# Layer 0 of a two-layer attention network: scores and values in groups of two steps, and the embedding's terms in one matmul

## The chip, the cores and the metric

The kernel runs on one core of one Trainium2 chip. The metric is the device time of one execution in microseconds (us); the time of a kernel is the median of its runs, and less is better. A core has a matmul engine (TensorE, "PE" in the profile, its weight loads listed apart as "PEld"), a vector engine (VectorE, "DVE"), an activation engine (ScalarE, "ACT"), a general engine (GpSimd, "POOL") and a queue that issues transfers (SyncE, "SP"). They run side by side and wait for one another through semaphores. SBUF is the working memory of 128 partitions; PSUM holds the results of matmuls, here in 8 banks of 128 x 512 float32.

## The reference

Two layers work on an input of 2 x 512 channels x 64 x 32 positions, that is 2048 positions per batch. Layer 0, the only one that the change touches, is softmax attention with 8 heads of 64 channels. Queries and keys get 64 extra input channels (32 that depend on the row alone, 32 that depend on the column alone):

```python
def _L0_conv_ref(hidden_states, Wq, Wk, Wv, Wout, bout):
    emb = get_embeddings(B, H, W, FREQ_DIM, TIME_DIM, ...)   # 32 rows of freq (by h), 32 of time (by w)
    qk_hs = jnp.concatenate([hidden_states, emb], axis=1)
    ...
    q = qk_hs @ Wq ; k = qk_hs @ Wk ; v = v_hs @ Wv          # 8 heads of 64
    scores = jnp.einsum('bhqd,bhkd->bhqk', q, k) * scale
    attn = jax.nn.softmax(scores, axis=-1)
    o = jnp.einsum('bhqk,bhkd->bhqd', attn, v)
    o = o @ Wout + bout
    return o + hidden_states
```

Layer 1 (a landmark attention with a pseudo-inverse, a convolution of 33 taps and a dequantised linear layer) follows, and takes more than half of the time. Its instructions are the same before and after the change. All arithmetic is float32.

## The kernel before

Layer 0 walks over 8 pairs of heads (2 batches x 4 pairs). For one pair, `q` and `k` lie in SBUF as 128 rows (64 per head) x 2048 positions, `v` as 16 tiles of 128 positions x 128. One step is a pair (t, c): t is one of 4 blocks of 512 queries, c one of 16 tiles of 128 keys, so there are 64 steps per pair and 512 in the layer. A step makes the scores of both heads, 64 rows of TensorE each, into one PSUM tile of two banks (two such tiles), and ScalarE's exponential into an SBUF tile `p` (4 buffers). The values part of the step multiplies `p` by `v`, 64 columns of TensorE for each head, into `av`, and VectorE adds `p` to `acc`, from which the sums of the softmax come at the end of a block of queries. The values of a step are issued after the scores of the next:

```python
ps      = tile_pool(bufs=2, space=PSUM)     # sc: 2 x 2 banks, av: 2 x 1, pp: 2 x 1
ppool   = tile_pool(name="pf0", bufs=4)     # p, and the squares of the layer norm
...
def scores(t, c):
    sc = ps.tile([P, 2, TB], F32, tag="sc")
    for h in range(2):
        rows = slice(h * D, (h + 1) * D)                       # D = 64
        nc.tensor.matmul(sc[:, h, :], lhsT=hd.k[rows, c * P : (c + 1) * P],
                         rhs=hd.q[rows, t * TB : (t + 1) * TB], start=True, stop=True)   # L881
    p = ppool.tile([P, 2, TB], F32, tag="p")
    nc.scalar.activation(p, sc, AF.Exp, scale=D**-0.5)                                   # L889
    return p

for i in range(len(steps) + 1):
    p = scores(*steps[i]) if i < len(steps) else None
    if pending is not None:
        (t, c), pp = pending
        if c == 0:
            av = ps.tile([P, TB], F32, tag="av"); acc = apool.tile([P, 2, TB], F32, tag="acc")
        for h in range(2):
            half = slice(h * D, (h + 1) * D)
            nc.tensor.matmul(av[half, :], lhsT=hd.v[:, c, half], rhs=pp[:, h, :],
                             start=c == 0, stop=c == NST - 1)                            # L903
        if c == 0: first = pp
        else:      nc.vector.tensor_tensor(acc, first if c == 1 else acc, pp, ALU.add)   # L909
        if c == NST - 1:
            rs = bank(...)                                                 # two matmuls, L913
            nc.vector.reciprocal(rinv, rs)                                               # L917
            nc.vector.tensor_tensor(hd.q[:, t * TB : (t + 1) * TB], av, rinv, ALU.mult)  # L918
    pending = (steps[i], p) if p is not None else None
    while done * len(steps) < n_filler * (i + 1) and next(filler, filler) is not filler:
        done += 1
```

The fillers are pieces of other work, so that they lie between steps: 15 units that make `q`, `k` and `v` of the next pair of heads, and, while the first pair of batch 1 runs, 24 units that finish batch 0 (output projection `yp` and layer norm). The projections use the whole 128 x 128 array:

```python
fp = bank(...)                                      # the embedding's terms
nc.tensor.matmul(fp[:, :H], lhsT=we[kind][:, 0, cols], rhs=femb, ...)           # 32 rows, L756
nc.tensor.matmul(fp[:, H:H + W], lhsT=we[kind][:, 1, cols], rhs=temb, ...)      # 32 rows, L757
...                                                 # DVE copy, POOL spreads the sum over 64 x 32
for k in range(KC):                                 # 4 matmuls per 512 positions, L773
    nc.tensor.matmul(pp, lhsT=w_sb[kind][:, k, cols], rhs=xbs[t][:, k, :], ...)
nc.vector.tensor_tensor(dst[:, toks], pp, e[:, toks], ALU.add)                  # L776
...
mean  = matmul(mean_w, total)                       # finish: L841, after POOL's sums (L814)
xn    = xb - mean                                   # DVE, L843
sq    = POOL: squares and their sum                 # L849 to L851, two buffers of ppool
var   = matmul(mean_w, sq)                          # L854
rstd  = apool.tile([P, TB], F32, tag="rstd", bufs=1)   # ACT Sqrt, DVE reciprocal, POOL product
```

The scheduler of the language may move an instruction ahead of its neighbours on the same engine; it did so for some scores, whose two heads then stand apart.

Of the kernel before, what the change touches and what calls it, by code (L numbers as in the profile page):

```python
# [10 lines left out]
F32 = mybir.dt.float32  # L11
I32 = mybir.dt.int32
AF = mybir.ActivationFunctionType
ALU = mybir.AluOpType
AX = mybir.AxisListType

P = 128
B, C, H, W = 2, 512, 64, 32
S = H * W
KC = C // P  # L20
HEADS, D = 8, 64
NPAIR = HEADS // 2
TB = 512
NTB = S // TB
NST = S // P
# [628 lines left out]

SAFE = 60.0


@with_exitstack
def layer0(
# [20 lines left out]
    nc = tc.nc  # L680
    const = ctx.enter_context(tc.tile_pool(name="const0", bufs=1))
    small = ctx.enter_context(tc.tile_pool(name="small0", bufs=2))
    ps = ctx.enter_context(tc.tile_pool(name="ps0", bufs=2, space=bass.MemoryType.PSUM))
    wpool = ctx.enter_context(tc.tile_pool(name="wf0", bufs=1))
# [1 line left out]
    epool = ctx.enter_context(tc.tile_pool(name="ef0", bufs=1))  # L686
    qopool = ctx.enter_context(tc.tile_pool(name="qof0", bufs=NPAIR + 1))
    kvpool = ctx.enter_context(tc.tile_pool(name="kvf0", bufs=2))
    ppool = ctx.enter_context(tc.tile_pool(name="pf0", bufs=4))
    apool = ctx.enter_context(tc.tile_pool(name="af0", bufs=2))  # L690
    lpool = ctx.enter_context(tc.tile_pool(name="lf0", bufs=1))

# [3 lines left out]
    def bank(name):  # L696
        return ps.tile([P, 512], F32, tag="pp", name=name)
# [3 lines left out]
    ones = const.tile([P, D], F32, name="ones_f")  # L701
# [9 lines left out]
    nc.sync.dma_start(b0_sb, b0)  # L711
    bound = const.tile([P, B * NPAIR], F32, name="bound0")

    femb = const.tile([32, H], F32, name="femb")
    nc.sync.dma_start(femb, freq)
    temb = const.tile([32, W], F32, name="temb")
    nc.sync.dma_start(temb, time)
    w_sb, we = {}, {}
    for kind, w in (("q", wq0), ("k", wk0)):
        w_sb[kind] = wpool.tile([P, KC, C], F32, name=f"w{kind}_f")  # L720
        nc.sync.dma_start(w_sb[kind], chunked(w[:C, :]))
        we[kind] = wpool.tile([32, 2, C], F32, name=f"we{kind}_f")
        nc.sync.dma_start(we[kind], w[C:, :].rearrange("(s p) n -> p s n", p=32))

    def load_x(b):
        tiles = []
# [12 lines left out]
    class Heads:  # L739
# [6 lines left out]
        def units(self):  # L746
            cols = slice(self.hp * P, (self.hp + 1) * P)
            xbs = self.xbs
            self.q = qopool.tile([P, S], F32, tag="qo", name=f"q_{self.name}")
            self.k = kvpool.tile([P, S], F32, tag="k", name=f"k_{self.name}")  # L750
            self.v = kvpool.tile([P, NST, P], F32, tag="v", name=f"v_{self.name}")

            def embedded(kind):

                fp = bank(f"fp_{kind}_{self.name}")
                nc.tensor.matmul(fp[:, :H], lhsT=we[kind][:, 0, cols], rhs=femb, start=True, stop=True)  # L756
                nc.tensor.matmul(fp[:, H : H + W], lhsT=we[kind][:, 1, cols], rhs=temb, start=True, stop=True)  # L757
                ft = small.tile([P, H + W], F32, tag="ft", name=f"ft_{kind}_{self.name}")
                nc.vector.tensor_copy(ft, fp[:, : H + W])
                e = epool.tile([P, H, W], F32, tag="e", name=f"e_{kind}_{self.name}")  # L760
                nc.gpsimd.tensor_tensor(
                    e,
                    ft[:, :H].unsqueeze(2).to_broadcast([P, H, W]),
                    ft[:, H:].unsqueeze(1).to_broadcast([P, H, W]),
                    ALU.add,
                )
                return e.rearrange("p h w -> p (h w)")

            def project(kind, dst, e, t):
                toks = slice(t * TB, (t + 1) * TB)  # L770
                pp = bank(f"pp_{kind}_{self.name}_{t}")
                for k in range(KC):
                    nc.tensor.matmul(  # L773
                        pp, lhsT=w_sb[kind][:, k, cols], rhs=xbs[t][:, k, :], start=k == 0, stop=k == KC - 1
                    )
                nc.vector.tensor_tensor(dst[:, toks], pp, e[:, toks], ALU.add)  # L776

            def values(t):
                vp = bank(f"vp_{self.name}_{t}")
                for j in range(4):  # L780
                    for k in range(KC):
                        nc.tensor.matmul(
                            vp[:, j * P : (j + 1) * P],
                            lhsT=xbs[t][:, k, j * P : (j + 1) * P],
                            rhs=wv_sb[:, k, cols],
                            start=k == 0,
                            stop=k == KC - 1,
                        )
                nc.scalar.copy(self.v[:, 4 * t : 4 * t + 4, :], vp.rearrange("p (j d) -> p j d", d=P))

            for kind, dst in (("q", self.q), ("k", self.k)):
                e = embedded(kind)
                yield
                for t in range(NTB):
                    project(kind, dst, e, t)
                    yield
            for t in range(NTB):
                values(t)
                yield

            big = small.tile([P, 2], F32, tag="big", name=f"big_{self.name}")
            for i, m in enumerate((self.q, self.k)):
                nc.vector.tensor_reduce(big[:, i : i + 1], m, AX.X, ALU.max, apply_absolute_value=True)
            i = self.b * NPAIR + self.hp
            nc.vector.tensor_tensor(bound[:, i : i + 1], big[:, :1], big[:, 1:], ALU.mult)
            yield
# [10 lines left out]
    def finish_units(b, oTs):  # L817

        for t in range(NTB):
            toks = slice(t * TB, (t + 1) * TB)  # L820
            name = f"f0_{b}_{t}"
            xb = lpool.tile([P, KC, TB], F32, tag="xr", name=f"xr_{name}")
            nc.sync.dma_start(xb, chunked(x[b])[:, :, toks])
            for m in range(KC):
                yp = bank(f"yp_{name}_{m}")
                for k in range(NPAIR):
                    nc.tensor.matmul(
                        yp,
                        lhsT=wo_sb[:, k, m * P : (m + 1) * P],
                        rhs=oTs[k][:, toks],  # L830
                        start=k == 0,
                        stop=k == NPAIR - 1,
# [19 lines left out]
            var = bank(f"var_{name}")  # L852
            for j in range(2):
                nc.tensor.matmul(var, lhsT=mean_w, rhs=sq[:, j, :], start=j == 0, stop=j == 1)  # L854
            rstd = apool.tile([P, TB], F32, tag="rstd", name=f"rstd_{name}", bufs=1)
            nc.scalar.activation(rstd, var, AF.Sqrt, bias=eps, scale=1.0)
            nc.vector.reciprocal(rstd, rstd)
            nc.gpsimd.tensor_tensor(
# [13 lines left out]
    def attention(hd, filler, n_filler):  # L872

        steps = [(t, c) for t in range(NTB) for c in range(NST)]
        av, acc, done = None, None, 0

        def scores(t, c):
            sc = ps.tile([P, 2, TB], F32, tag="sc", name=f"sc_{hd.name}_{t}_{c}")
            for h in range(2):
                rows = slice(h * D, (h + 1) * D)  # L880
                nc.tensor.matmul(  # L881
                    sc[:, h, :],
                    lhsT=hd.k[rows, c * P : (c + 1) * P],
                    rhs=hd.q[rows, t * TB : (t + 1) * TB],
                    start=True,
                    stop=True,
                )
            p = ppool.tile([P, 2, TB], F32, tag="p", name=f"p_{hd.name}_{t}_{c}")
            nc.scalar.activation(p, sc, AF.Exp, scale=D**-0.5)  # L889
            return p  # L890

        pending = None
        first = None
        for i in range(len(steps) + 1):
            p = scores(*steps[i]) if i < len(steps) else None
            if pending is not None:
                (t, c), pp = pending
                if c == 0:
                    av = ps.tile([P, TB], F32, tag="av", name=f"av_{hd.name}_{t}")
                    acc = apool.tile([P, 2, TB], F32, tag="acc", name=f"acc_{hd.name}_{t}")  # L900
                for h in range(2):
                    half = slice(h * D, (h + 1) * D)
                    nc.tensor.matmul(  # L903
                        av[half, :], lhsT=hd.v[:, c, half], rhs=pp[:, h, :], start=c == 0, stop=c == NST - 1
                    )
                if c == 0:
                    first = pp
                else:
                    nc.vector.tensor_tensor(acc, first if c == 1 else acc, pp, ALU.add)  # L909
                if c == NST - 1:  # L910
                    rs = bank(f"rs_{hd.name}_{t}")
                    for h in range(2):
                        nc.tensor.matmul(  # L913
                            rs[h * D : (h + 1) * D, :], lhsT=ones, rhs=acc[:, h, :], start=True, stop=True
                        )
                    rinv = apool.tile([P, TB], F32, tag="rinv", name=f"rinv_{hd.name}_{t}", bufs=1)
                    nc.vector.reciprocal(rinv, rs)  # L917
                    nc.vector.tensor_tensor(hd.q[:, t * TB : (t + 1) * TB], av, rinv, ALU.mult)  # L918
            pending = (steps[i], p) if p is not None else None
            while done * len(steps) < n_filler * (i + 1) and next(filler, filler) is not filler:  # L920
                done += 1
        for _ in filler:
            pass
# [137 lines left out]
```

## Time and profile before

| | |
|---|---|
| time, median of 3 runs | 4262.48 us (4260.63 to 4263.36) |
| span of the profiled execution | 4266.9 us |
| TensorE matmuls, busy | 3966.1 us, 93% |
| VectorE, ScalarE, GpSimd, busy | 42%, 26%, 8% |
| scores (L881), values (L903), records | 2048 each |
| exponentials (L889) | 512, 1024 ns each |
| additions to `acc` (L909) | 448 of 1320 ns mean |

The page gives the busy time of each engine, the chain of work that ended last, and groups of instructions by line. A float32 matmul shows as two records of TensorE, each about half of its work, so a pair of heads has four records per step. Two matmuls on different rows or columns of the array may have records that start together. The end of a record is modelled, so the time that TensorE spends on something is read from the start of one record to the start of the next. In the timeline the columns are the start, the length, engine, line, operation, output and inputs, the part of the array (rows*columns) and the shape, the number of records merged, and in brackets the idle time ahead and who ended it.

### The profile page before, as it was taken

How to read it: one execution, taken by the hardware profiler on the slowest of the kernel's cores; microseconds unless marked ns; L12 is line 12 of the kernel's file. 1: busy time of each engine (PE TensorE's matmuls, PEld its weight loads, DVE VectorE, ACT ScalarE, POOL GpSimd, SP SyncE). 2: the span in 40 equal slices, each digit the busy share in tenths (PEclk: the TensorE clock that was granted, in tenths of full speed). 3: DMA queues.
4: the chain of work that ended last, by engine and by line, in shares of the span. 5: the costliest groups of instructions: out<-in, count | busy, mean ns of one | idle time of the engine just before them, and what ended most of it. 6: DMA issues, size and time to landing. Idle time of an engine off the chain costs nothing.

```text
span 4266.9 us, 42948 instructions
## 1 busy us (share of the span) xinstructions
PE 3966.1 (93%) x18002; PEld 2285.3 (54%) x18002; DVE 1808.6 (42%) x2393; ACT 1113.8 (26%) x1760; POOL 326.8 (8%) x200
## 2 busy tenths in 40 slices
PE   8999999989999995379999999899999789999987
PEld 3333233323332322258888888577677347677743
DVE  3565655565555562463333333224323214323322
ACT  1333333322333440012212211123223103223210
POOL 1000000132000004530000000000000100000001
PEclk9999999999999997679999999899999999999999
DMA  2000010010000002300000000100010010000010
GB/s 92 1 1 1 1 40 1 30 59 30 1 1 1 1 1 89 90 0 1 1 1 1 1 1 1 62 1 8 1 50 30 30 35 8 8 1 1 11 50 31
DMA packets 48970, 81.92 MB, mean 19 GB/s; under 512 B 3584, under 2 KB 22016, under 8 KB 48768
## 3 DMA queue, kind: packets, MB, share of 16 engines
q1 hardware_dynamic: 42240, 53.92, 3.9%
q0 software_dynamic: 6528, 25.17, 1.6%
q8 instruction: 144, 2.36, 0.2%
q14 instruction: 58, 0.48, 0.0%
HBM read 52.34 MB, written 26.74 MB: 19 GB/s over the span
## 4 chain that ended last, share of the span: by engine, by line
PE 80%; issue 9%; POOL 4%; DVE 3%; DMA 1%; ACT 1%; SPq 0%; POOLq 0%; ACTq 0%; DVEq 0%
PE sc_f L881 10%; PE av_f L903 9%; PE pr_a L437 4%; PE pr_b L437 4%; PE pr_c L437 4%; PE pr_z L437 4%; PE acc L599 4%; PE sc L113 3%; PE sc L568 3%; PE pp_q_f L773 3%; PE acc L607 3%; PE av L134 3%; PE pp_q L169 3%; PE vp L183 3%; PE pp_k L169 3%
## 5 line engine op out<-in xcount | busy, mean ns | idle before, releaser
L909 DVE TENSOR_TENSOR acc_f<-acc_f,p_f 128x1024 f32<-128x1024 f32 x448 | 591.6, 1320 | 427.6 <-ACT p_f L889 421.0
L889 ACT ACTIVATE p_f<-sc_f 128x1024 f32<-128x1024 f32 x512 | 524.1, 1024 | 828.9 <-PE sc_f L881 825.5
L881 PE MATMUL sc_f<-q_f,k_f 64*128 64x512 f32 x2048 | 596.1, 644 | 0.0
L903 PE MATMUL av_f<-p_f,v_f 128*64 128x512 f32 x2048 | 555.3, 619 | 0.8 <-ACT p_f L889 0.6
L881 PEld LDWEIGHTS sc_f<-q_f,k_f 64*128 64x128 f32 x2048 | 159.0, 185 | 393.6 <-issue 389.5
L903 PEld LDWEIGHTS av_f<-p_f,v_f 128*64 128x64 f32 x2048 | 101.7, 135 | 393.4 <-issue 362.8
L599 PEld LDWEIGHTS acc<-v,band 128*128 128x128 f32 x1472 | 176.9, 193 | 5.7 <-issue 4.6
L599 PE MATMUL acc<-v,band 128*128 128x64 f32 x1472 | 178.5, 270 | 0.0
L437 PE MATMUL pr_a<-z,xT 128*128 128x256 f32 x768 | 174.8, 382 | 2.0 <-DVE z L463 2.0
L645 PE MATMUL fp<-xn,mT 128*128 128x512 f32 x256 | 132.1, 681 | 45.0 <-POOL xn L162 45.0
L437 PE MATMUL pr_b<-m,aT 128*128 128x256 f32 x768 | 173.7, 379 | 0.0
L437 PE MATMUL pr_c<-m,aT 128*128 128x256 f32 x768 | 169.7, 379 | 0.0
L113 PE MATMUL sc<-kT,qL 64*128 64x512 f32 x256 | 146.6, 711 | 13.6 <-ACT p L119 13.6
L437 PEld LDWEIGHTS pr_c<-m,aT 128*128 128x128 f32 x768 | 145.9, 190 | 19.8
L437 PEld LDWEIGHTS pr_a<-z,xT 128*128 128x128 f32 x768 | 143.7, 192 | 20.7 <-DVE z L463 2.7
L114 DVE TENSOR_REDUCE mx<-sc 128x1 f32<-128x512 f32 x128 | 88.6, 692 | 151.3 <-PE sc L113 151.3
L437 PEld LDWEIGHTS pr_b<-m,aT 128*128 128x128 f32 x768 | 142.2, 190 | 17.4
L449 ACT COPY zT<-tp 128x512 f32<-128x512 f32 x80 | 43.0, 588 | 408.7 <-PE tp L447 408.7
L169 PE MATMUL pp_q<-xh,w_c 128*128 128x512 f32 x256 | 121.3, 616 | 23.5 <-DMA w_c<-in_wqkv_dram 23.5
L437 PE MATMUL pr_z<-m,zT 128*128 128x256 f32 x640 | 141.4, 379 | 0.0
L614 DVE RECIPROCAL rs<-acc 128x2 f32<-128x2 f32 x128 | 21.9, 171 | 279.2 <-ACT o L612 279.2
L607 PE MATMUL acc<-u,pT 128*128 128x65 f32 x1024 | 137.4, 276 | 0.0
(182 smaller groups left out, 5160.8 us busy)
## 6 DMA issues: line engine op xcount, KB each, us to landing
xf<-in_x_dram SPq DMA_DIRECT2D x8, 1024.0 KB, 8.8
xr_f<-in_x_dram SPq DMA_DIRECT2D x8, 1024.0 KB, 5.0
x_fd<-xr_f POOLq DMA_DIRECT2D x8, 1024.0 KB, 4.6
xh_fd<-xn_f POOLq DMA_DIRECT2D x8, 1024.0 KB, 4.6
xh<-xh_fd SPq DMA_DIRECT2D x8, 1024.0 KB, 6.4
x<-x_fd SPq DMA_DIRECT2D x8, 1024.0 KB, 6.2
out_dram<-x POOLq DMA_DIRECT2D x8, 1024.0 KB, 4.6
w_c<-in_wqkv_dram SPq DMA_DIRECT2D x24, 256.0 KB, 3.8
```

Of the source, the lines that this page charges most:

```text
L113: nc.tensor.matmul(sc, lhsT=q_ap, rhs=k_ap[:, j * 512 : (j + 1) * 512], start=True, stop=True)
L134: nc.tensor.matmul(av[:, : D + 1], lhsT=pT[:, c, :], rhs=v_of(c), start=c == 0, stop=c == nch - 1)
L169: nc.tensor.matmul(pp, lhsT=w_of(k), rhs=r_of(k), start=k == 0, stop=k == nk - 1)
L183: nc.tensor.matmul(vp[:, j * P : (j + 1) * P], lhsT=x_of(t)[:, k, j * P : (j + 1) * P], rhs=w_of(k), start=k == 0, stop=k == KC - 1,)
L437: nc.tensor.matmul(pr[:, t, :], lhsT=lhsT[:, k, t * P : (t + 1) * P], rhs=rhs[:, k, :], start=k == 0, stop=k == 1,)
L599: nc.tensor.matmul(conv[:, h * D : (h + 1) * D], lhsT=band[:, 2 * hp + h, lo : lo + P], rhs=v[:, c, h, :D], start=c == near[0], stop=c == ...
L607: nc.tensor.matmul(av[:, h, :], lhsT=pT[:, h, t, c, :], rhs=u[:, h, c, :], start=c == 0, stop=c == 1,)
L645: nc.tensor.matmul(fp, lhsT=mT[:, k, m * P : (m + 1) * P], rhs=xn[:, k, :], start=k == 0, stop=k == KC - 1,)
L881: nc.tensor.matmul(sc[:, h, :], lhsT=hd.k[rows, c * P : (c + 1) * P], rhs=hd.q[rows, t * TB : (t + 1) * TB], start=True, stop=True,)
L889: nc.scalar.activation(p, sc, AF.Exp, scale=D**-0.5)
L903: nc.tensor.matmul(av[half, :], lhsT=hd.v[:, c, half], rhs=pp[:, h, :], start=c == 0, stop=c == NST - 1)
L909: nc.vector.tensor_tensor(acc, first if c == 1 else acc, pp, ALU.add)
```

## The change

Scores and values are issued in groups of two steps: the scores of two steps in a row, then the values of the two steps before them. The pool of `p` gets a fifth buffer, for which the layer norm's `rstd` now shares a buffer with `rinv`. The embedding's two matmuls of 32 rows become one of 64 rows: the two small tables lie on the diagonal of one tile that holds zeros elsewhere, and the weights are loaded as 64 rows.

```diff
+GROUP = 2
...
-    ppool = ctx.enter_context(tc.tile_pool(name="pf0", bufs=4))
+    ppool = ctx.enter_context(tc.tile_pool(name="pf0", bufs=5))
...
-    femb = const.tile([32, H], F32, name="femb")
-    nc.sync.dma_start(femb, freq)
-    temb = const.tile([32, W], F32, name="temb")
-    nc.sync.dma_start(temb, time)
+    emb_sb = const.tile([64, H + W], F32, name="emb_f")
+    nc.vector.memset(emb_sb, 0.0)
+    nc.sync.dma_start(emb_sb[:32, :H], freq)
+    nc.sync.dma_start(emb_sb[32:, H:], time)
...
-        we[kind] = wpool.tile([32, 2, C], F32, name=f"we{kind}_f")
-        nc.sync.dma_start(we[kind], w[C:, :].rearrange("(s p) n -> p s n", p=32))
+        we[kind] = wpool.tile([64, C], F32, name=f"we{kind}_f")
+        nc.sync.dma_start(we[kind], w[C:, :])
...
-                nc.tensor.matmul(fp[:, :H], lhsT=we[kind][:, 0, cols], rhs=femb, start=True, stop=True)
-                nc.tensor.matmul(fp[:, H : H + W], lhsT=we[kind][:, 1, cols], rhs=temb, start=True, stop=True)
+                nc.tensor.matmul(fp[:, : H + W], lhsT=we[kind][:, cols], rhs=emb_sb, start=True, stop=True)
...
-            rstd = apool.tile([P, TB], F32, tag="rstd", name=f"rstd_{name}", bufs=1)
+            rstd = apool.tile([P, TB], F32, tag="rinv", name=f"rstd_{name}", bufs=1)
...
-        for i in range(len(steps) + 1):
-            p = scores(*steps[i]) if i < len(steps) else None
-            if pending is not None:
-                (t, c), pp = pending
-                ...                    # the values part, as above
-            pending = (steps[i], p) if p is not None else None
-            while done * len(steps) < n_filler * (i + 1) and next(filler, filler) is not filler:
+        def values(step, pp):
+            ...                        # the same values part, now a function
+        pending = []
+        for i in range(0, len(steps) + 1, GROUP):
+            group = steps[i : i + GROUP]
+            made = [(step, scores(*step)) for step in group]
+            for step, pp in pending:
+                values(step, pp)
+            pending = made
+            while done * len(steps) < n_filler * (i + GROUP) and next(filler, filler) is not filler:
                 done += 1
```

More of the change, by code (lines that the diff above doesn't have):

```diff
@@ L890, in scores @@
             return p
-        pending = None
-        first = None
-        for i in range(len(steps) + 1):
-            p = scores(*steps[i]) if i < len(steps) else None
-            if pending is not None:
-                (t, c), pp = pending
[L898 to L918, printed above, removed]
-            pending = (steps[i], p) if p is not None else None
-            while done * len(steps) < n_filler * (i + 1) and next(filler, filler) is not filler:
@@ new lines, in values @@
+        def values(step, pp):
+            nonlocal av, acc, first
+            t, c = step
+            if c == 0:
+                av = ps.tile([P, TB], F32, tag="av", name=f"av_{hd.name}_{t}")
+                acc = apool.tile([P, 2, TB], F32, tag="acc", name=f"acc_{hd.name}_{t}")
+            for h in range(2):
+                half = slice(h * D, (h + 1) * D)
+                nc.tensor.matmul(
+                    av[half, :], lhsT=hd.v[:, c, half], rhs=pp[:, h, :], start=c == 0, stop=c == NST - 1
+                )
+            if c == 0:
+                first = pp
+            else:
+                nc.vector.tensor_tensor(acc, first if c == 1 else acc, pp, ALU.add)
+            if c == NST - 1:
+                rs = bank(f"rs_{hd.name}_{t}")
+                for h in range(2):
+                    nc.tensor.matmul(
+                        rs[h * D : (h + 1) * D, :], lhsT=ones, rhs=acc[:, h, :], start=True, stop=True
+                    )
+                rinv = apool.tile([P, TB], F32, tag="rinv", name=f"rinv_{hd.name}_{t}", bufs=1)
+                nc.vector.reciprocal(rinv, rs)
+                nc.vector.tensor_tensor(hd.q[:, t * TB : (t + 1) * TB], av, rinv, ALU.mult)
```

## The prediction

> **What bounds the kernel now.** I read the shares of busy time first, then the chain of work that ended last, and then the groups by line.
>
> ```profile
> PE 3966.1 (93%) x18002; PEld 2285.3 (54%) x18002; DVE 1808.6 (42%) x2393; ACT 1113.8 (26%) x1760; POOL 326.8 (8%) x200
> PE 80%; issue 9%; POOL 4%; DVE 3%; DMA 1%; ACT 1%; SPq 0%; POOLq 0%; ACTq 0%; DVEq 0%
> L909 DVE TENSOR_TENSOR acc_f<-acc_f,p_f 128x1024 f32<-128x1024 f32 x448 | 591.6, 1320 | 427.6 <-ACT p_f L889 421.0
> L889 ACT ACTIVATE p_f<-sc_f 128x1024 f32<-128x1024 f32 x512 | 524.1, 1024 | 828.9 <-PE sc_f L881 825.5
> L881 PE MATMUL sc_f<-q_f,k_f 64*128 64x512 f32 x2048 | 596.1, 644 | 0.0
> L903 PE MATMUL av_f<-p_f,v_f 128*64 128x512 f32 x2048 | 555.3, 619 | 0.8 <-ACT p_f L889 0.6
> ```
>
> TensorE sets the end: it is on 80% of the chain, and scores and values have next to no idle time ahead of them, while ScalarE waits for scores and VectorE for ScalarE. So layer 0's attention gets shorter only if TensorE needs less time for the same matmuls. Does it waste any? The timeline of TensorE about 601 us shows it, in narrow stretches so that records which start together stand on a line of their own:
>
> ```profile
> 601.03 0.60 PE L903 MATMUL av_f<-p_f,v_f 128*64 128x512 f32 x2
> 601.56 0.70 PE L881 MATMUL sc_f<-q_f,k_f 64*128 64x512 f32 x2
> ...
> 602.09 0.59 PE L881 MATMUL sc_f<-q_f,k_f 64*128 64x512 f32 x2
> 602.62 0.65 PE L903 MATMUL av_f<-p_f,v_f 128*64 128x512 f32 x2
> ```
>
> Both heads run at once, in two rounds of two records. The starts of the rounds of one step are 601.56 and 602.09 (scores), 602.62 and about 603.10 (values; the step before had 600.55 and 601.03), and the next scores start at 603.63: intervals of 0.53, 0.53, 0.48 and 0.53 us, 2.07 in all. A round alone is cheaper. The same timeline, wider, at the end of a block of queries and at a projection:
>
> ```profile
> 603.63 1.12 PE L881 MATMUL sc_f<-q_f,k_f 64*128 64x512 f32 x2
> 604.68 1.08 PE L903 MATMUL av_f<-p_f,v_f 128*64 128x512 f32 x4
> 605.59 1.03 PE L913 MATMUL rs_f<-acc_f,ones_f 128*64 128x512 f32 x4
> 606.55 1.12 PE L881 MATMUL sc_f<-q_f,k_f 64*128 64x512 f32 x2
> 607.60 0.43 PE L756 MATMUL fp_q_f<-femb,weq_f 32*128 32x64 f32 x2
> 607.87 0.35 PE L757 MATMUL fp_q_f<-temb,weq_f 32*128 32x32 f32 x2
> 608.16 1.13 PE L881 MATMUL sc_f<-q_f,k_f 64*128 64x512 f32 x4
> ...
> 616.43 3.70 PE L773 MATMUL pp_q_f<-xf,wq_f 128*128 128x512 f32 x8
> 620.06 1.13 PE L881 MATMUL sc_f<-q_f,k_f 64*128 64x512 f32 x4
> ```
>
> From values to `rs` (604.68 to 605.59), both 64 columns wide, is 0.91 us, where values to scores take 1.01; so the last round before a neighbour of the same shape takes 0.91 - 0.48 = 0.43 instead of 0.53. The base is then 0.427 us a round. A change of the array's shape costs two things: about 0.10 at the end of the old shape, and at the start of the new one the weight load, about 0.107 for 128 columns of weights (scores, projections) and 0.053 for 64 (values). The sum agrees: 4 x 0.427 + 2 x 0.10 + 0.107 + 0.053 = 2.07; and for the projection 8 x 0.427 + 0.10 + 0.107 = 3.62 against 616.43 to 620.06 = 3.63.
>
> The lines at 603.63 and 606.55 show a second waste: the two heads of one score, torn apart by the scheduler, take 1.05 each, as long as both together.
>
> **What the Trainium skill says.** The page "TensorEngine Tiling (Array Packing)", section Key Properties, says that changing the tiling mode drains TensorE; the trace agrees, with 0.10 us. The page "TensorE: Matmul & The Clock Gate", section LDWEIGHTS, gives P/1.2 ns for P columns, so 107 ns and 53 ns, as found above. Its Part 2, step 1, says that weight loads are pulled ahead of running matmuls; within one shape the trace agrees (no load shows in the 0.43 from values to `rs`), after a change of shape it doesn't. The page "FP8 and Floating Point Precision" says that true FP32 takes 4 passes; two rounds of 0.427 are 4 x 512 columns at 0.417 ns, which agrees.
>
> **The change, part by part.**
>
> *Changes of shape.* I count them in the order of TensorE's instructions in the two built programs, over layer 0, taking scores (64 rows), values and `rs` (64 columns), whole-array work, and before also the 32-row embedding as shapes. Into scores: 524 before, 257 after. Into values: 512 and 248. Into whole-array work: 111 and 105. Into the 32-row form: 15 and none, as the 64-row form has the shape of the scores. At 0.207, 0.153, 0.207 and 0.207 us each, before is 108.5 + 78.3 + 23.0 + 3.1 = 212.9 us, after 53.2 + 37.9 + 21.7 = 112.8. Saved: 100 us. The work is all on the path. A group of two steps should take 8 x 0.427 + 0.36 = 3.78 us instead of 4.14.
>
> *Torn scores.* 13 before, of which 7 at the joint of two pairs of heads; 6 after. 7 x 0.853 = 6 us saved.
>
> *Embedding.* 607.60 to 608.16 is 0.56, less the 0.21 of the shape is 0.35. After, two rounds each bounded by a weight load of 0.107, some 0.21. Over 16: 2 us saved.
>
> *The turn of the batch.* Here TensorE waits for the layer norm:
>
> ```profile
> 822.75 2.80 POOL L849 TENSOR_TENSOR sq_f<-xn_f 128x1024 f32<-128x1024 f32 x1 [3.58 <-DVE xn_f L843]
> 831.72 3.62 PE L854 MATMUL var_f<-sq_f,mean_wf 128*128 128x512 f32 x4 [5.18 <-POOL sq_f L851]
> 800.00:1000.00 200.00, 174.24 (x483) 52.21 (x482) 122.73 (x68) 54.90 (x53) 79.67 (x33) 0.91 0.16 60
> ```
>
> The chain from `mean` over VectorE and GpSimd to `var` has the same length after. In the new order there is some 0.7 to 2.5 us less attention work between `mean` and `var`, four times, both by the grouping and as the same steps run faster: I put 1.3 us each, 5 us lost. In the 200 us of the last line (busy us and counts of PE, PEld, DVE, ACT, POOL, then the clock) the mean clock was 0.91, so there a few us more or less hang on when the clock falls.
>
> *What moves beside.* Start, end of the layer and layer 1 keep their instructions; the memset ahead of the small tables is far from the first transfer that TensorE waits for. I put zero.
>
> Sum: 100 + 6 + 2 - 5 = 103 us; 4262.5 - 103 = 4159.5.
>
> **The rivals.**
>
> *A new wait of scores for ScalarE.* There are still two score tiles. The second score of a group starts about 0.96 after the first; the exponentials, which started 1.18 us after their scores before (601.56 and 602.74), end at about 2.2 and 3.25 us of the group, the next scores need their tiles at 3.8 and 4.7. Slack of 1.4 us or more, so I don't expect it. If each second score waited for its tile, it would show as ACT ahead of L881; 0.36 us would suffice to eat the gain: 4260.
>
> *A weight load that isn't pulled ahead,* because the second score carries a wait on ScalarE. Projections that wait for VectorE's release of their bank show no gap at the change of banks, which speaks against. If so, 256 x 0.107 = 27 us come back: 4187.
>
> *VectorE or the buffers of `p` become the bound.* Two additions of 1.23 us per group of 3.78 leave a third of it free. The bottleneck would be after each block, where the reciprocal (3.36 us), product (0.69) and first addition (up to 1.8) come one after another: 6 us in which no `p` is freed. With five buffers the sixth exponential needs its buffer about 6.0 us after `rs`, when its score is ready at about 5.7, and the next user of its tile comes 2 us later. If it stalled by 1 us in each of 32 blocks: 4190.
>
> *The gain is smaller for lack of room elsewhere,* a turn of the batch that loses 15 us with its clock: 4170.
>
> **Range and chances.** The main term is a count times an interval that repeats exactly in the trace, so I give the sum most of the weight. The turn of the batch and the unknown layout of memory are worth some 10 us each way; the second and third rival, some 27 us, have a chance of about one in twelve together. That gives 4147 to 4181. Faster by over 2% means below 4179: 0.90. Within 2%: 0.09. Slower: 0.01.
>
> **What would show it.** In the timeline: `sc` x8 and `av` x8 alternating, with a group at 3.78 us (starts of rounds 0.53, 0.43, 0.43, 0.53, then 0.48, 0.43, 0.43, 0.53); mean of L881 near 615 ns and of L903 near 605, since half the records lose the weight load; ScalarE and VectorE with the same means and less idle time; the waits at L854 longer by a us or two. The prediction is wrong if the second score of a group starts later than 0.96 us after the first, if L881 or L903 show idle time with ACT or DVE as releaser, or if the turn of the batch grows by more than 15 us.

## The result, and the profile after

The changed kernel takes 4163.69 us (median; 4163.25 to 4164.2), the kernel before 4261.95 us beside it. The ratio is 0.9769, with a 95% interval of 0.9753 to 0.9786: 98 us less. The prediction was 4159.5 us, range 4147 to 4181.

The head of the page after: shares of busy time, the chain that ended last, and the same four groups as were shown of before (the lines of the file have moved: L907 was L909, L890 was L889, L882 was L881, L901 was L903).

```profile
PE 3857.8 (93%) x17970; PEld 2326.4 (56%) x17970; DVE 1814.3 (44%) x2394; ACT 1085.6 (26%) x1760; POOL 330.0 (8%) x200
PE 80%; issue 9%; POOL 5%; DVE 4%; ACT 1%; DMA 1%; SPq 0%; POOLq 0%; ACTq 0%; DVEq 0%
L907 DVE TENSOR_TENSOR acc_f<-acc_f,p_f 128x1024 f32<-128x1024 f32 x448 | 607.5, 1356 | 290.9 <-ACT p_f L890 266.2
L890 ACT ACTIVATE p_f<-sc_f 128x1024 f32<-128x1024 f32 x512 | 496.7, 1021 | 722.0 <-PE sc_f L882 714.7
L882 PE MATMUL sc_f<-q_f,k_f 64*128 64x512 f32 x2048 | 518.2, 616 | 0.7 <-ACT p_f L890 0.3
L901 PE MATMUL av_f<-p_f,v_f 128*64 128x512 f32 x2048 | 494.1, 604 | 0.0
```

TensorE is still 93% busy and 80% of the chain: the page's shares tell nothing of what happened. The counts are the same, and the mean of a record of scores fell from 644 to 616 ns, of values from 619 to 604. VectorE's additions have not become fewer; their idle time ahead fell from 427.6 to 290.9 us, as the chain from scores over exponentials now feeds them faster. Their mean did not stay the same, as was forecast, but rose from 1320 to 1356 ns; TensorE shows no wait for them.

The timeline of TensorE about 620 us shows where it comes from. These are narrow stretches again, so that each line is one round of both heads:

```profile
619.58 0.70 PE L882 MATMUL sc_f<-q_f,k_f 64*128 64x512 f32 x2
620.11 0.60 PE L882 MATMUL sc_f<-q_f,k_f 64*128 64x512 f32 x2
620.54 0.60 PE L882 MATMUL sc_f<-q_f,k_f 64*128 64x512 f32 x2
620.97 0.59 PE L882 MATMUL sc_f<-q_f,k_f 64*128 64x512 f32 x2
...
621.50 0.65 PE L901 MATMUL av_f<-p_f,v_f 128*64 128x512 f32 x2
621.98 0.60 PE L901 MATMUL av_f<-p_f,v_f 128*64 128x512 f32 x2
622.41 0.60 PE L901 MATMUL av_f<-p_f,v_f 128*64 128x512 f32 x2
```

The rounds of scores are 0.53, 0.43, 0.43 and 0.53 us apart, those of values start with 0.48 and 0.43. A round inside a group costs 0.43; only the first (its weight load) and the last (the end of the old shape) are longer. Before, a step had no round that was neither first nor last. The same stretch, wider:

```profile
615.79 1.99 PE L882 MATMUL sc_f<-q_f,k_f 64*128 64x512 f32 x8
617.71 1.94 PE L901 MATMUL av_f<-p_f,v_f 128*64 128x512 f32 x8
619.58 1.99 PE L882 MATMUL sc_f<-q_f,k_f 64*128 64x512 f32 x8
621.50 1.94 PE L901 MATMUL av_f<-p_f,v_f 128*64 128x512 f32 x8
623.36 0.35 PE L758 MATMUL fp_k_f<-emb_f,wek_f 64*128 64x96 f32 x1
623.38 0.69 PE L882 MATMUL sc_f<-q_f,k_f 64*128 64x512 f32 x1
623.55 0.27 PE L758 MATMUL fp_k_f<-emb_f,wek_f 64*128 64x96 f32 x1
623.66 1.91 PE L882 MATMUL sc_f<-q_f,k_f 64*128 64x512 f32 x7
```

From 615.79 to 619.58 two steps take 3.79 us, where they took 4.14. The embedding's one matmul lies among scores of the same shape: its stretch up to the next values (625.50 in the same timeline) is 2.14 us instead of 1.92 (619.58 to 621.50), so it costs 0.22.

The first and last start of scores give the length of all attention. First of before, then of after (shortest, median and longest record, then first and last start):

```profile
L881 PE MATMUL sc_f<-q_f,k_f x2048: 589/693/1220, 60.3 to 1584.8; 64*128 64x512 f32 x187
```

```profile
L882 PE MATMUL sc_f<-q_f,k_f x2048: 589/589/1219, 60.4 to 1478.8; 64*128 64x512 f32 x187
```

1524.5 us became 1418.4: 106.1 us, the whole difference of the two profiled spans (4266.9 and 4161.6). That is more than the 98 of the medians, because the profiled execution of before took 4269.0 us, 7 above its median, and that of after 4163.68, just its median; so the gain is 98 to 106 us. Nothing came from the rest of the program, which takes 2682 us after the last score in both traces; in all the runs below it varies from 2679 to 2685. A length of attention is therefore a finer measure than a time. The median record, 693 before and 589 after, fell because before every second record holds a weight load and after every fourth (589 + 104/2 and 589 + 104/4 give means of 641 and 615 ns, and 644 and 616 were measured).

The traces also give each pair of heads by itself, from its first score to the first of the next pair. Five ordinary pairs take 182.1 us each before and 169.1 after; the pair that runs at the turn of the batch takes 299.5 and 283.7.

At the turn of the batch TensorE's waits on other engines, between 740 and 1010 us, are these; before, then after:

```profile
PE var_f L854 <- POOL sq_f L851: 20.0, 4, 6.6
PE mean_f L841 <- POOL s_xf L814: 4.1, 3, 1.5
PE rs_f L913 <- DVE acc_f L909: 1.2, 1, 1.2
PE av_f L903 <- ACT p_f L889: 0.4, 1, 0.4
```

```profile
PE var_f L855 <- POOL sq_f L852: 21.9, 4, 5.7
PE mean_f L842 <- POOL s_xf L815: 7.0, 4, 1.8
```

25.7 us became 28.9. But a wait is not all that the turn costs. In the clock records of the traces TensorE's clock is at half for part of that time (34.1 us before, 30.7 after, between 700 and 1010 us), and its work then takes twice as long: in the trace of after, weight loads of `var` start at 781.07 and 781.92, 0.85 us apart, where 0.43 is usual. Half of this time, without the part in which TensorE waited anyway (6.0 and 9.7 us), is lost by the clock: an estimate of 14.1 us before and 10.5 after. Waits and clock together are 39.8 us before and 39.4 after, so by this estimate the turn costs the same.

### The profile page after: what moved, and what is told of

It reads as the page before. It is cut to its first block, busy times and chain, and to the rows that moved or that the text cites. A ratio compares the mean times of both kernels' runs of the same rounds, so it can differ in the third digit from the quotient of the medians.

```text
span 4161.6 us, 42884 instructions
## 1 busy us (share of the span) xinstructions
PE 3857.8 (93%) x17970; PEld 2326.4 (56%) x17970; DVE 1814.3 (44%) x2394; ACT 1085.6 (26%) x1760; POOL 330.0 (8%) x200
## 4 chain that ended last, share of the span: by engine, by line
PE 80%; issue 9%; POOL 5%; DVE 4%; ACT 1%; DMA 1%; SPq 0%; POOLq 0%; ACTq 0%; DVEq 0%
PE sc_f L882 9%; PE av_f L901 9%; PE pr_a L437 4%; PE pr_b L437 4%; PE pr_c L437 4%; PE pr_z L437 4%; PE acc L599 4%; PE sc L113 3%; PE sc L568 3%; PE acc L607 3%; PE av L134 3%; PE pp_q L169 3%; PE vp L183 3%; PE pp_q_f L774 3%; PE pp_k L169 3%
## 5 line engine op out<-in xcount | busy, mean ns | idle before, releaser
L907 DVE TENSOR_TENSOR acc_f<-acc_f,p_f 128x1024 f32<-128x1024 f32 x448 | 607.5, 1356 | 290.9 <-ACT p_f L890 266.2
L890 ACT ACTIVATE p_f<-sc_f 128x1024 f32<-128x1024 f32 x512 | 496.7, 1021 | 722.0 <-PE sc_f L882 714.7
L882 PE MATMUL sc_f<-q_f,k_f 64*128 64x512 f32 x2048 | 518.2, 616 | 0.7 <-ACT p_f L890 0.3
L901 PE MATMUL av_f<-p_f,v_f 128*64 128x512 f32 x2048 | 494.1, 604 | 0.0
L882 PEld LDWEIGHTS sc_f<-q_f,k_f 64*128 64x128 f32 x2048 | 181.7, 186 | 299.3 <-issue 189.2
L901 PEld LDWEIGHTS av_f<-p_f,v_f 128*64 128x64 f32 x2048 | 124.8, 136 | 338.8 <-issue 336.5
L113 PE MATMUL sc<-kT,qL 64*128 64x512 f32 x256 | 146.5, 711 | 13.6 <-ACT p L119 13.6
```

Source lines behind the costliest of these rows:

```text
L113: nc.tensor.matmul(sc, lhsT=q_ap, rhs=k_ap[:, j * 512 : (j + 1) * 512], start=True, stop=True)
```

## The experiments

The theory is that the gain is a count of changes of the array's shape times a fixed cost. The rivals are that the longer distance between a score and its values removed a wait for ScalarE, that the fifth buffer brought it, or that the embedding did. Each run below is named with its median and its ratio to the kernel before, measured beside it on the same chip (4262.92 us for the first four, 4262.68 for the rest; it was 4261.95 beside the changed kernel, so times of different sets compare to about 1 us).

**Without the grouping.** All else of the change stays.

```diff
-GROUP = 2
+GROUP = 1
```

> The change without its grouping: one step per group, but five buffers of p and the embedding in one matmul. Changes of the array's shape are the cause: 1143 of them in the instruction order, 208.9 us by the same costs, against 212.9 before; with one torn score less and 2 us for the embedding that makes 4255 us. If the fifth buffer or the embedding brought the gain: near 4164 us.

Measured: 4259.99 us, ratio 0.9993 (0.9986 to 1.0). So the fifth buffer, the shared `rstd` and the embedding bring next to nothing by themselves; the grouping is the change. The 96.3 us between this kernel and the changed one stand against 96.0 from the two counts (208.9 - 112.9). That fit is closer than it deserves to be, for six more torn scores (12 against 6) make another 5 us, and the turn costs 1 us less here (23.9 us of waits and 14.4 by the clock, against 28.9 and 10.5). So the terms give 100 us; in the traces, where scores last 1517.8 us here and 1418.4 in the changed kernel, it is 99. Its steps have the old form:

```profile
607.53 1.13 PE L882 MATMUL sc_f<-q_f,k_f 64*128 64x512 f32 x4
608.59 1.08 PE L901 MATMUL av_f<-p_f,v_f 128*64 128x512 f32 x4
609.60 1.13 PE L882 MATMUL sc_f<-q_f,k_f 64*128 64x512 f32 x4
```

2.07 us a step, as before.

**The grouping alone.** The changed kernel with the embedding and the buffers put back:

```diff
-    ppool = ctx.enter_context(tc.tile_pool(name="pf0", bufs=5))
+    ppool = ctx.enter_context(tc.tile_pool(name="pf0", bufs=4))
...
-                nc.tensor.matmul(fp[:, : H + W], lhsT=we[kind][:, cols], rhs=emb_sb, start=True, stop=True)
+                nc.tensor.matmul(fp[:, :H], lhsT=we[kind][:, 0, cols], rhs=femb, start=True, stop=True)
+                nc.tensor.matmul(fp[:, H : H + W], lhsT=we[kind][:, 1, cols], rhs=temb, start=True, stop=True)
...                                      # so too the two tables, the load of the weights, and rstd
```

> The grouping alone: the kernel before with groups of two, four buffers of p and the embedding's two matmuls of 32 rows. Changes of shape are the cause: 630 of them, 117.0 us, so 95.9 us saved, 5 us by torn scores, 5 us lost at the turn of the batch: 4166 us, 2 to 4 us above the changed kernel. If the fifth buffer is needed (VectorE late after each block): 4180 to 4190 us.

Measured: 4166.97 us, ratio 0.9771 (0.9754 to 0.9787), as the theory expected. The grouping needs neither the fifth buffer nor the new embedding. One term of the expectation was wrong: this order of instructions lost nothing at the turn of the batch, where TensorE waited 19.9 us in place of 25.7:

```profile
PE mean_f L843 <- POOL s_xf L816: 12.3, 4, 3.3
PE var_f L856 <- POOL sq_f L853: 7.6, 3, 4.4
```

Nor did it gain the difference, for its clock was at half for 41.0 us there, so that by the same estimate 18.8 us are lost by the clock, against 14.1. The turn costs 39 us in place of 40, and the terms give 95.9 + 5 + 1 = 102. Scores last from 60.1 to 1482.4 us in its profile, which is 102 us less than before; the medians differ by 96.

**The same distance without groups.** Scores and values alternate step by step, but the values are those of two steps before:

```diff
-        for i in range(0, len(steps) + 1, GROUP):
+        for i in range(0, len(steps) + DEPTH, GROUP):      # GROUP = 1, DEPTH = 2
...
-            for step, pp in pending:
-                values(step, pp)
-            pending = made
+            pending = pending + made
+            while len(pending) > DEPTH or (pending and not made):
+                values(*pending.pop(0))
```

> The changed kernel with scores and values alternating step by step, but the values two steps behind the scores, as far apart as in the groups. Changes of shape are the cause: 1114 of them, 203.7 us, 9 us less than before, with torn scores and the embedding some 4245 to 4250 us. If the gain came from the longer distance between a score and its values, so that nobody waits for ScalarE: near 4164 us.

Measured: 4242.35 us, ratio 0.9945 (0.9926 to 0.9965). One of the four executions took 6120 us at a mean clock of 0.62 in place of 0.96; the median of the other three is 4240.7 us. The distance is not the cause: with it alone 77 of the 98 us are missing. What it did bring is 9 us by the count, some 6 by seven torn scores fewer than before, some 2 by the embedding, and 10 at the turn of the batch (19.0 us of waits and 10.7 by the clock, in place of 25.7 and 14.1); that is 27, where scores last 25 us less than before in the trace (1499.6 against 1524.5) and the time is 22 less. In the timeline the steps are still 2.07 us apart:

```profile
606.07 1.13 PE L883 MATMUL sc_f<-q_f,k_f 64*128 64x512 f32 x4
607.13 1.08 PE L902 MATMUL av_f<-p_f,v_f 128*64 128x512 f32 x4
608.14 1.13 PE L883 MATMUL sc_f<-q_f,k_f 64*128 64x512 f32 x4
```

**Four buffers.** The changed kernel with one buffer of `p` less, and `rstd` in a buffer of its own:

```diff
-    ppool = ctx.enter_context(tc.tile_pool(name="pf0", bufs=5))
+    ppool = ctx.enter_context(tc.tile_pool(name="pf0", bufs=4))
...
-            rstd = apool.tile([P, TB], F32, tag="rinv", ..., bufs=1)
+            rstd = apool.tile([P, TB], F32, tag="rstd", ..., bufs=1)
```

> The changed kernel with four buffers of p instead of five (and rstd in a buffer of its own). If the buffers don't bind: 4164 to 4167 us, with the same 610 changes of shape. If the chain of reciprocal, product and first addition after each of the 32 blocks holds the exponentials, and they the scores: 1 us each, 4190 us or more.

Measured: 4162.31 us, ratio 0.9764 (0.9747 to 0.978), no different from the changed kernel's 4163.69. The buffers don't bind. In the traces every pair of heads takes as long as in the changed kernel, 169.1 us and at the turn 283.7, though TensorE waits 20.3 us there and not 28.9: what it waits less, it loses by the clock (an estimate of 18.6 us against 10.5). Beside the grouping alone, this run also gives the worth of the embedding: 4166.97 - 4162.31 = 4.7 us by the medians, whose ranges touch (4164.11 to 4169.31, 4160.06 to 4165.11), and 4.0 by the length of attention (1422.3 and 1418.3 us).

**Fillers two at a time.** If a change of shape costs what it is said to, fewer visits to the whole-array shape must pay as well:

```diff
-            while done * len(steps) < n_filler * (i + GROUP) and next(filler, filler) is not filler:
-                done += 1
+            while (done + 1) * len(steps) < n_filler * (i + GROUP):
+                for _ in range(2):
+                    next(filler, None)
+                done += 2
```

> The changed kernel with the fillers issued two at a time. Changes of shape are the cause: 576 instead of 610, 105.8 us instead of 112.9, 7 us less, 4157 us. If two fillers in a row wait for VectorE or ScalarE to release their banks: no gain or a loss, 4164 us or more.

Measured: 4155.92 us, ratio 0.9751 (0.9735 to 0.9767): 7.8 us below the changed kernel's 4163.69, with 7.0 expected. In the traces attention is 5.7 us shorter (1412.7 against 1418.4); scores waited 1.9 us for ScalarE in place of 0.3, so the count promises 5.4. So the mechanism holds at the visits to the whole-array shape too, and the closer fit of the medians is luck.

**Groups of three.** By the count it should be better still; the two score tiles say no.

```diff
-GROUP = 2
+GROUP = 3
...
-    ppool = ctx.enter_context(tc.tile_pool(name="pf0", bufs=5))
+    ppool = ctx.enter_context(tc.tile_pool(name="pf0", bufs=6))
...
-        for i in range(0, len(steps) + 1, GROUP):
-            group = steps[i : i + GROUP]
+        groups = [
+            [(t, c) for c in range(lo, min(lo + GROUP, NST))] for t in range(NTB) for lo in range(0, NST, GROUP)
+        ]
...
+        for group in groups + [[]]:
...                                      # acc gets one buffer in place of two, for the room
```

> Groups of three steps (five of three and one of one in a block of 16), six buffers of p, acc with one buffer. By the count of changes of shape alone, 483 and 89.8 us, it would be 23 us faster than groups of two: 4137 us. But there are two score tiles: the third score of a group has to wait for the first exponential, some 0.4 us in each of 160 groups, 70 us: 4205 us, with idle time ahead of the scores put down to ScalarE.

Measured: 4224.28 us, ratio 0.9908 (0.9891 to 0.9924), 61 us slower than groups of two. The timeline of all engines (weight loads and VectorE left out here) shows the wait:

```profile
604.18 1.99 PE L882 MATMUL sc_f<-q_f,k_f 64*128 64x512 f32 x8
...
605.36 1.94 ACT L890 ACTIVATE p_f<-sc_f 128x1024 f32<-128x1024 f32 x2 [6.39 <-PE sc_f L882]
...
606.44 1.13 PE L882 MATMUL sc_f<-q_f,k_f 64*128 64x512 f32 x4 [0.27 <-ACT p_f L890]
607.50 2.79 PE L901 MATMUL av_f<-p_f,v_f 128*64 128x512 f32 x12
```

The first exponential starts at 605.36 and takes 1.02, so it ends at 606.38; the third score starts at 606.44, 2.26 us after the first, where it could have started after 0.53 + 3 x 0.43 = 1.82. The wait is 0.44, as expected (the 0.27 in brackets is less, as it counts from the modelled end of the record before). But the expectation was 19 us too low, for the third score then takes 1.06 (606.44 to 607.50) and not 0.96: its weight load, 0.107, isn't hidden, although the shape has not changed. 160 x 0.107 = 17 us. The trace has 137 groups of three whose six rounds of scores stand uninterrupted, and their intervals are alike: medians of 0.53, 0.43, 0.43, 0.86, 0.53 and 0.53 us. The values last until a projection at 610.22, so a group takes 3.32 + 2.72 = 6.04 us for three steps, against 3 x 1.893 = 5.68 in groups of two.

**Work at the turn of the batch.** Empty fillers between the steps of the layer norm, so that attention lies there:

```diff
             total = summed(xb, f"x{name}")
+            yield
             mean = bank(f"mean_{name}")
...
-            sq = ppool.tile([P, 2, TB], F32, tag="p", name=f"sq_{name}")
+            sq = lpool.tile([P, 2, TB], F32, tag="sq", name=f"sq_{name}")
...
             nc.gpsimd.tensor_tensor(sq, sq, sq2, ALU.add)
+            for _ in range(3):
+                yield
             var = bank(f"var_{name}")
...
-    N_FINISH = NTB * (KC + 2)
+    N_FINISH = NTB * (KC + 6)      # and acc with one buffer, for the room
```

> The changed kernel with empty fillers at the turn of the batch: one ahead of the mean, three ahead of the variance, so that attention steps lie beside the layer norm's work on VectorE and GpSimd (the squares get a buffer of their own, acc one buffer). TensorE waits 28.9 us there in the changed kernel, and its clock is halved in about 31 us of it. If these are plain waits: 4130 to 4138 us. If VectorE or ScalarE then holds the attention steps: 4150 us or more.

Measured: 4137.3 us, ratio 0.9707 (0.9691 to 0.9724): 26 us below the changed kernel. TensorE's waits between 700 and 1010 us fell from 28.9 to 12.5:

```profile
PE mean_f L843 <- POOL s_xf L815: 6.1, 4, 1.8
PE var_f L858 <- POOL sq_f L853: 4.4, 2, 2.3
PE pp_q_f L774 <- DVE q_f L777: 2.0, 1, 2.0
```

In attention the trace shows a gain of 23.6 us, all of it in the pair at the turn (260.1 us in place of 283.7), and the waits are 16 of it. The busy lines of both kernels for the 300 us about the turn, after and then this one (stretch, length, busy time of PE, PEld, DVE, ACT and POOL with counts, the clock of TensorE, transfers), show that the clock rose from 0.95 to 0.98 as well:

```profile
700.00:1000.00 300.00, 271.11 (x946) 103.46 (x946) 188.20 (x120) 85.58 (x88) 82.30 (x34) 0.95 0.12 42
```

```profile
700.00:1000.00 300.00, 287.24 (x1080) 113.35 (x1078) 193.71 (x127) 94.06 (x98) 82.57 (x34) 0.98 0.12 42
```

0.03 of 300 us would be 9 us, but in the changed kernel 9.7 us of the halved time were waits and are counted among them already; by the estimate used above 6.7 us are lost by the clock in place of 10.5, a gain of 4. Seven changes of shape fewer in the trace make another 1.4. That is some 22 of the 23.6 us; what the buffers of `sq` and `acc` do by themselves was not tested.

**Both.** The last two edits in one kernel.

> Both of the former together: empty fillers at the turn and fillers two at a time. 576 changes of shape. If the two gains add: 4125 to 4132 us. If a pair of fillers undoes the distance at the turn (two empty ones at once): near 4145 us.

Measured: 4136.63 us, ratio 0.9704 (0.9688 to 0.9721). Neither case of the expectation came: the gains don't add in the time, where the two medians differ by less than the runs of either, and the distance at the turn isn't undone. In the profiles scores end at 1455.1 us in the run before and at 1451.3 us in this one, so 4 us of the 5.6 that the count promises (603 changes of shape against 576) are there, but both spans are 4134 us: the rest of the program took 2679.2 us there and 2682.9 here. The 4 us are seen in six pairs of heads, which take 168.5 us each in place of 169.1, just as with the fillers in pairs and no work at the turn; the pair at the turn takes 260.1 us either way. So the gain of the ordinary pairs is real, and the time, with the spread of the rest, is too coarse to show it.

## Why the prediction was right

*Changes of shape, 100 us predicted.* Right in mechanism and size. The starts of rounds are those that were forecast, a group takes 3.79 us against a forecast 3.78, the mean records 616 and 604 ns against 615 and 605. The medians fit the bare counts better than they should (96.3 us for 96.0 with the grouping reverted, 96.0 for 95.9 with it alone, 7.8 for 7.0 with fillers in pairs), as other terms happen to cancel. With these put in, the lengths of attention are 99 for 100, 102 for 102 and 5.7 for 5.4. In an ordinary pair of heads the trace has 143 changes of shape before and 74 after; with one torn score and two embeddings the predicted costs give 13.6 us, and 13.0 were saved in each. That the parts of the cost are a drain and a weight load that isn't hidden remains a reading: the intervals at both ends of a group show two costs at two places, 0.10 and 0.05 or 0.107, and the latter go with the columns of the weights, but no run took one of them away alone.

*Torn scores, 6 us.* Not tested by themselves. They moved with the order of instructions in several runs, and the sums with them agree with the traces to 2 us.

*Embedding, 2 us.* The cost after was right, 0.22 us against 0.21. In all it is worth some 4 us (4.7 by the medians, 4.0 in the traces), where the 2 of the matmul and 4 in the count (630 changes of shape with the old form, 610 without) promised 6.

*The turn of the batch, 5 us lost.* Not borne out in the traces, of which there is one for each kernel. The waits grew by 3.2 us, 1.9 of them ahead of `var`, where they were forecast, but less was lost by the clock, and the pair at the turn saved 15.8 us, more than an ordinary one. In the run with the grouping alone the waits even fell. Waits by themselves don't measure this turn; only waits and clock together do, and they came to 39 to 40 us in all the runs in groups of two without work at the turn, as in the kernel before.

*The rivals.* A wait of scores for ScalarE doesn't appear in groups of two (0.3 us in all), and appears at once in groups of three. The weight load that isn't pulled ahead was rightly put aside for a wait that is long over, and it is real for a wait that is not. VectorE after each block doesn't bind even with four buffers; the estimate that the sixth exponential would be tight was too careful. One sum there is off: a loss of 0.36 us in each of 256 groups is 92 us, which would give about 4252 us and not 4260.

*The sum.* 103 us predicted, 98.3 measured by the medians, 105.3 between the two profiled executions. Without the term for the turn the sum is 108, for 106.1 of attention in the traces. So the shape term is confirmed, while that 103 fits the medians to 5 us is partly luck: one term of 5 us was not there, and the two measures of the gain differ by 8. The 4 us between prediction and time lie inside what executions of the kernel before differ by (4257.56 to 4269.46 us in the later runs).

## What to carry to other kernels

When TensorE alternates between shapes of its array (half its rows, half its columns, all of it), look at the intervals between starts of records, not at the busy share, and count the changes: here each cost 0.15 to 0.21 us, and two of them added a fifth to a step of 1.71 us of work. Issue as many matmuls of one shape in a row as the PSUM tiles between the engines allow, and no more: with two score tiles two steps were the best of one, two and three, and a third met the exponential. Then look at the places where the filler work itself waits; here four pauses of a layer norm were worth another 26 us for a few empty steps. Count there what the halved clock takes beside the waits, and for gains of a few us compare the stretch that changed, not the time of the whole program.

## What was not expected of the hardware

A score that has to wait for ScalarE also pays for its weight load, 0.107 us for 128 columns, though the array's shape stays the same (third score of a group of three: 1.06 us from its start to that of the values, against 0.96 for the same two rounds in a row). At the turn of the batch less waiting brought no time: with four buffers TensorE waited 8.6 us less than in the changed kernel, its clock was at half for 41.0 us in place of 30.7, and the pair of heads took 283.7 us in both. Why the clock fell for longer stays open. A matmul of 64 rows placed among scores of 64 rows costs about what was estimated for its two rounds, and no change of shape: 0.22 us, with its records starting between those of the scores (623.36, 623.38, 623.55, 623.66).
